# The last four steps of an attention kernel: biases, one output and one sum moved to other places in the engines' queues

## The chip, the cores and the metric

The kernel runs on one core of one Trainium2 chip. Its time is the device time of one execution in microseconds, given as the median over runs. TensorE (PE), VectorE (DVE), ScalarE (ACT), GpSimd (POOL) and SyncE (SP) each work through a queue of instructions in order; SyncE issues most of the transfers.

## The reference

Attention over 8 batches of 512 tokens with 512 features, in 16 heads of 32, all in float32, with a conditioning row added to queries and keys, and the input added to the output:

```python
Q, K, V = split(x @ Wq.T + bq), split(x @ Wk.T + bk), split(x @ Wv.T + bv)
cQ = Q + split(cond @ Wq.T + bq)          # one row per batch, added to all tokens
cK = K + split(cond @ Wk.T + bk)
attn = softmax(einsum('bhqd,bhkd->bhqk', cQ, cK) / sqrt(32))
out = x + merge(einsum('bhqk,bhkd->bhqd', attn, V))
```

## The kernel before

The work is cut into 32 steps, t = 0 to 31: four heads of one batch each, which fill the 128 partitions. One step needs the row maxima of its scores, the exponentials, the product with V, the denominators, and an output of 128 x 512 numbers, in which 32 x 32 blocks are transposed on VectorE. Steps are staggered: while step t takes its exponentials, the scores of step t+1 are made and their maxima taken, and the projections of the next batch run. The order of every engine's instructions is the order in which the code issues them; waits are placed by the framework from what an instruction reads and writes. The eight banks of PSUM are dealt out by a table (`TURNS`, `row`, `at_end`), so the reader of a bank decides when its next writer may start.

The change lies in the end, from step 29 on (`t = T - 3`), where no projections are left. The names and lines that it and the prediction touch:

- `crossed(t, kc, qc, u)` gives TensorE, in turns, the scores of step t for the exponentials of key chunk kc (L1192, L1195) and those of step u for its maxima of query chunk qc (L635). ScalarE takes the exponentials (L1211), VectorE the maxima: two by one head (L1213), then two heads at once (L644).
- `split_max` splits the negated maxima into three bfloat16 parts: a cast, a subtraction, a cast, a subtraction (L696 to L699). `transpose_max` turns them on TensorE (L722) and copies them out (L728); a matmul with ones then adds them to the scores (L738 in `exponentials`, whose score matmuls are L741 and whose exponentials are L752).
- `times_v` (L763) multiplies exponentials by V. `part_of` does so for some key chunks, and its sum leaves PSUM at once: the first time by a copy on ScalarE into `parts[t]` (L1022), the second time by a copy on ScalarE into a spare place (L1016) and an addition on GpSimd (L1017).
- Denominators: up to step 29 they are sums that ScalarE made beside its exponentials; `masked` (GpSimd, L790) and `spread_sums` (TensorE, L800) lay them out and `denominators_of` copies them from PSUM (ScalarE, L1027). For steps 30 and 31 the exponentials of the four key chunks are added (`sum_of`: L1167 for the first two chunks, L1169 for each further one, on VectorE but for one half of step 30, on GpSimd), and `times_ones` (TensorE, L773) adds over the keys. Of step 31, chunks 0 to 2 are added first and chunk 3 goes to TensorE as it is.
- `send_parts(t, den)`: reciprocal (VectorE, L1032), then `send`: transposed (VectorE, L830), multiplied by the reciprocal (GpSimd, L831), added to the input in `xr[t]` (GpSimd, L832). `store` issues four transfers on SyncE (L850).
- `add_bias(u)` adds V's bias to the input `xr[u]` (GpSimd, L209).
- Step 30's output is made by VectorE alone (transposes L1287 and L1292, reciprocal L1290, multiplication L1294, addition of the input L1326) in `y30`, and stored by `store_30` (L1299), two transfers on SyncE and two on ScalarE's queue.
- Step 31's output: the input times the denominators (L1309) is added to the product (L1319, in two halves), TensorE turns it back (L1321) and the denominators too (L854, from a copy that ScalarE makes, L1311); reciprocal (L1329) and multiplication (L1334, two halves) follow, and four transfers (L1341).

Of the kernel before, what the change touches and what calls it, by code (L numbers as in the profile page):

```python
# [12 lines left out]
ALU = mybir.AluOpType  # L13
# [4 lines left out]
def kernel(  # L18
# [38 lines left out]
    nc = tc.nc  # L57
# [5 lines left out]
    HG = P // HD  # L63
    NP = HG // 2
    NS = S // P
# [56 lines left out]
    def banks(i, n=1):  # L122

        row = row_of[0] or [at_end[j] for j in TURNS[turn[0]]]
        j = row[i]
        if n == 1:
            return psum[:, j, :]
        k = row[i + 1]
        return psum[:, j : k + 1 : k - j, :]
# [27 lines left out]
    def spread(a, d, n=1):  # L157

        return a.rearrange("(f j) d -> j f d", j=BL)[:, :, d : d + n * BL]
# [18 lines left out]
    def turned_by_vector(t):  # L178

        return t < T - 1  # L180

    def load_residual(t):

        b, g = divmod(t, G)
        if t == T - 1:

            xr[t] = xT[b][:, g, :]
        elif late:
            xr[t] = late_part(t % 2 * 10 + 2).rearrange("p (f e) -> p f e", e=BL)
            for h in range(HG):  # L190
                nc.sync.dma_start(xr[t][h * BL : (h + 1) * BL], spread(x[b], h * P + g * BL))
        else:
            two = op.tile([P, NB, 2, BL], F32, tag="xr", name=f"xr_{t}", bufs=2)
            twos[t // 2] = two
            for h in range(HG):
                nc.sync.dma_start(
                    two[h * BL : (h + 1) * BL].rearrange("p f c e -> p f (c e)"),
                    spread(x[b], h * P + g * BL, 2),
                )
            for i in range(2):  # L200
                xr[t + i] = two[:, :, i, :]

    def add_bias(t):

        if turned_by_vector(t):
            bias = bvs[:, t % G, :].unsqueeze(1).broadcast_to([P, NB, BL])
        else:
            bias = bvl.broadcast_to([P, S])
        nc.gpsimd.tensor_tensor(xr[t], xr[t], bias, ALU.add)  # L209
# [521 lines left out]
    es = {}  # L731
# [22 lines left out]
    def times_v(t, kc, pt, chunks=range(NS), half=None):  # L754
        b, g = divmod(t, G)
        at = slice(0, S) if half is None else slice(half * HS, (half + 1) * HS)
        cs = slice(0, NS) if half is None else slice(half * 2, half * 2 + 2)
        for j in range(HG):
            if t in BLOCKED:
                e = blocked[t][:, :, cs, j, kc * BL : (kc + 1) * BL].rearrange("p a c e -> p c a e")  # L760
            else:
                e = es[t, kc, j // 2][:, j % 2, at]
            nc.tensor.matmul(  # L763
                pt[j * HD : (j + 1) * HD, at],
                vs[b % 2][:, kc, (g * HG + j) * HD : (g * HG + j + 1) * HD],
                e,
                start=(kc == chunks[0]),
                stop=(kc == chunks[-1]),
            )

    def times_ones(of, pt, start, stop):
        for j in range(HG):
            nc.tensor.matmul(  # L773
                pt[j * HD : (j + 1) * HD, :],
                ones[:, :HD],
                of[j // 2][:, j % 2, :],
                start=start,
                stop=stop,
            )
# [18 lines left out]
    def spread_sums(apart, pd):  # L798
        for h in range(HG):
            nc.tensor.matmul(  # L800
                pd[h * BL : (h + 1) * BL, :NB],
                modulo,
                apart[:, h].rearrange("p c a -> p (c a)"),
                start=True,
                stop=True,
            )
# [31 lines left out]
    def store():  # L838
        while to_store:
            t = to_store.pop(0)  # L840
            b, g = divmod(t, G)
            for h in range(HG):
                r = slice(h * BL, (h + 1) * BL)
                if t < T - 4:
                    nc.sync.dma_start(
                        spread(out[b], h * P + (g - 1) * BL, 2),
                        twos[t // 2][r].rearrange("p f c e -> p f (c e)"),
                    )
                else:
                    nc.sync.dma_start(spread(out[b], h * P + g * BL), xr[t][r])  # L850

    def untranspose(o, pt):
        for qc in range(NS):
            nc.tensor.transpose(  # L854
                pt[:, qc * P : (qc + 1) * P], o[:, qc * P : (qc + 1) * P], ident
            )
# [143 lines left out]
    parts = {}  # L1000
# [3 lines left out]
    def late_part(i):  # L1004
        return late[0][:, i, :]

    def part_of(t, pt, of, between=None):

        for k, kc in enumerate(of):
            if k and between:  # L1010
                between()
            times_v(t, kc, pt, of)
        if t in parts:
            p = late_part(3 + len(parted))
            parted.append(t)
            nc.scalar.copy(p, pt)  # L1016
            nc.gpsimd.tensor_tensor(parts[t], parts[t], p, ALU.add)  # L1017
        else:
            if not parts:
                parts["all"] = stage.tile([P, NC, D], F32, tag="w", name="parts")  # L1020
            parts[t] = parts["all"][:, t % NC, :]
            nc.scalar.copy(parts[t], pt)  # L1022

    def denominators_of(t, pd):

        den = op.tile([P, NB, 1], F32, tag="den", name=f"den_{t}")
        nc.scalar.copy(den, pd[:, :NB].unsqueeze(2))  # L1027
        return den

    def send_parts(t, den):  # L1030
        rec = op.tile([P, NB, 1], F32, tag="recs", name=f"recs_{t}")
        nc.vector.reciprocal(rec, den)  # L1032
        send(t, parts[t], rec)
# [130 lines left out]
    def sum_of(t, to, kc, on, prs=range(NP)):  # L1164
        for pr in prs:
            if kc == 1:
                on.tensor_tensor(to[pr], es[t, 0, pr], es[t, 1, pr], ALU.add)  # L1167
            else:
                on.tensor_tensor(to[pr], to[pr], es[t, kc, pr], ALU.add)  # L1169
# [5 lines left out]
    def row(i):  # L1175
        turn[0] = 8 + i
# [41 lines left out]
    late.append(room("late").rearrange("p g c h s -> p (g c) (h s)"))  # L1218
    t = T - 3
    load_residual(t + 1)  # L1220
    row(4)
    exponentials(t, 0)
    row_max(t + 1, 1)
# [3 lines left out]
    den = denominators_of(t - 1, banks(3))  # L1227
# [7 lines left out]
    row(3)  # L1235
    crossed(t, 3, 0, t + 2)
    part_of(t, banks(2), [0, 1], lambda: transpose_max(t + 1, banks(3), nc.scalar.copy))
    add_bias(t - 1)
    send_parts(t - 1, den)
    store()  # L1240

    t = T - 2
    row(0)
    crossed(t, 0, 1)
    apart = masked(t - 1)
    load_residual(t + 1)
    for u in (t - 1, t, t + 1):
        add_bias(u)
    part_of(t - 1, banks(2), [2, 3])
    spread_sums(apart, banks(1))  # L1250
    den = denominators_of(t - 1, banks(1))
    row(1)
    crossed(t, 1, 2)
    acc = room_for_sums(t)
    sum_of(t, acc, 1, nc.gpsimd, [1])
    part_of(t, banks(2), [0])
    send_parts(t - 1, den)
    store()
    row(2)
    crossed(t, 2, 3)  # L1260
    split_max(t + 1, nc.vector)
# [9 lines left out]
    t = T - 1  # L1271
# [7 lines left out]
    acc2 = room_for_sums(t)  # L1279
# [2 lines left out]
    times_v(t, 1, pv)  # L1282
    pd = bank(5)
    times_ones(acc, pd, True, True)
    sum_of(t, acc2, 2, nc.vector)
    den = late_part(9).rearrange("p (f e) -> p f e", e=BL)
    nc.vector.transpose(den.rearrange("p f e -> p (f e)"), pd)  # L1287

    rec = op.tile([P, NB, 1], F32, tag="recs", name=f"recs_{t - 1}")
    nc.vector.reciprocal(rec, den[:, :, 0:1])  # L1290
    y30 = late_part(13).rearrange("p (f e) -> p f e", e=BL)
    nc.vector.transpose(y30.rearrange("p f e -> p (f e)"), parts[t - 1])  # L1292
    x30 = xr.pop(t - 1)
    nc.vector.tensor_tensor(y30, y30, rec.broadcast_to([P, NB, BL]), ALU.mult)  # L1294

    def store_30(queue, hs):
        b, g = divmod(t - 1, G)
        for h in hs:
            queue.dma_start(spread(out[b], h * P + g * BL), y30[h * BL : (h + 1) * BL])  # L1299
# [2 lines left out]
    times_v(t, 2, pv)  # L1302
    pd = bank(7)
    times_ones(acc2, pd, True, False)
    times_ones([es[t, 3, pr] for pr in range(NP)], pd, False, True)
    times_v(t, 3, pv)

    part_x = late_part(10)
    nc.vector.tensor_tensor(part_x, pd, xr[t], ALU.mult)  # L1309
    den = late_part(11)  # L1310
# [3 lines left out]
    rec = op.tile([P, NS, HG, 1], F32, tag="rec", name="rec")  # L1314
    pi, po = bank(6), [bank(4), bank(2)]
    b, g = divmod(t, G)
    two = [slice(0, HS), slice(HS, S)]
    for i in range(2):
        nc.vector.tensor_tensor(oT[:, two[i]], pv[:, two[i]], part_x[:, two[i]], ALU.add)  # L1319
        for qc in (i * 2, i * 2 + 1):  # L1320
            nc.tensor.transpose(  # L1321
                po[i][:, qc * P : (qc + 1) * P], oT[:, qc * P : (qc + 1) * P], ident
            )
        if i == 0:
            untranspose(den, pi)
    nc.vector.tensor_tensor(y30, y30, x30, ALU.add)  # L1326
    store_30(nc.sync, (0, 1))
    store_30(nc.scalar, (2,))
    nc.vector.reciprocal(  # L1329
        rec, pi.rearrange("p (c h e) -> p c h e", c=NS, h=HG)[:, :, :, 0:1]  # L1330
    )
    for i in range(2):
        cs = slice(i * 2, i * 2 + 2)
        nc.vector.tensor_tensor(  # L1334
# [5 lines left out]
        for c in (i * 2, i * 2 + 1):  # L1340
# [1 line left out]
                out[b].rearrange("(c p) (h g e) -> c g p h e", p=P, h=HG, g=G)[c, g],  # L1342
                y[:, c].rearrange("p (h e) -> p h e", h=HG),
            )
    store_30(nc.scalar, (3,))


# [1 line left out]
_INS = [  # L1349
# [27 lines left out]
```

## Time and profile before

| | |
|---|---|
| time, median of 3 runs (lowest, highest) | 664.89 us (664.83, 665.09) |
| the profiled execution: its own time, its span | 664.89 us, 663.1 us |
| busy share of the span: PE, DVE, ACT, POOL | 98%, 87%, 82%, 51% |
| busy from 609.8 to 632.6 us: PE, DVE, ACT, POOL | 22.8, 16.5, 15.4, 9.0 of 22.8 us |
| 632.6 to 641.4 | 7.6, 7.4, 6.4, 7.9 of 8.8 us |
| 641.4 to 656.1 | 14.7, 14.1, 9.2, 0.0 of 14.7 us |
| 656.1 to 660.4 | 1.1, 2.4, 0.6, 0.0 of 4.3 us |

Times in the profile count from the start of the span. L with a number is a line of the kernel before. A line of a timeline gives start, duration, engine, line, operation, what is written from what, shape, how many instructions are merged, and in brackets the idle time before and what ended it. PEld is TensorE loading weights; SPq and ACTq are the queues from which SyncE and ScalarE issue transfers. A float32 matmul shows as two instructions, one for each of its passes. In the chain of waits, each piece is what the next one waited for.

### The profile page before, as it was taken

Reading aid. Unit: us, or ns where it says so; the run is one execution under the profiler, and the core shown is the slowest. Engines: PE = TensorE matmul, PEld = TensorE weight load, DVE = VectorE, ACT = ScalarE, POOL = GpSimd, SP = SyncE. Lnnn points to the kernel's source line nnn. Section 1 sums busy time; section 2 is a strip of 40 time slices with the busy share of each in tenths; the row PEclk is TensorE's granted clock in tenths of the full one; section 3 lists DMA queues with packets and bytes.
Section 4 is the critical chain, followed back from the end, with each engine's and each line's share of the span. In section 5 each row is a group of like instructions: output and inputs, shape, how many; then the busy total and the mean of one; then the engine's idle time right before and its main releaser. Section 6 shows DMA issues by size and latency. Waiting matters only on the chain.

```text
span 663.1 us, 22865 instructions
## 1 busy us (share of the span) xinstructions
PE 652.7 (98%) x9100; PEld 307.0 (46%) x9100; DVE 578.4 (87%) x845; ACT 543.2 (82%) x1391; POOL 338.0 (51%) x447
## 2 busy tenths in 40 slices
PE   8999999999999999999999999999999999999996
PEld 7454444544445444444544445444544545445431
DVE  5898988989798898979889898998979888897787
ACT  2479797888979888898989889798997978888673
POOL 5642543647537464565635664464744656352360
PEclk9999999999999999999999999999999999999998
DMA  9718548285665838657493865839476573830212
GB/s 210 147 33 211 119 109 211 66 219 118 158 168 123 208 73 222 132 138 184 106 223 74 205 151 129 197 75 233 95 180 154 131 185 67 214 89 16 44 33 33
DMA packets 140815, 90.86 MB, mean 137 GB/s; under 512 B 117436, under 2 KB 126308, under 8 KB 140708
## 3 DMA queue, kind: packets, MB, share of 16 engines
q1 hardware_dynamic: 132196, 73.78, 48.3%
q0 software_dynamic: 5568, 14.95, 8.8%
q8 instruction: 72, 1.18, 0.8%
q10 hardware_dynamic: 2944, 0.66, 0.5%
q14 instruction: 35, 0.29, 0.1%
HBM read 20.27 MB, written 8.39 MB: 43 GB/s over the span
## 4 chain that ended last, share of the span: by engine, by line
PE 94%; DVE 3%; issue 1%; DMA 1%; ACT 1%; ACTq 0%; DVEq 0%
PE psum L469 44%; PE psum L635 19%; PE psum L763 16%; PE psum L741 8%; PE psum L738 3%; PE psum L410 2%; DVE acc L1169 1%; DMA early<-in_x_dram 1%; DVE nmax L644 1%; PE psum L1195 1%; DVE nmax L1213 0%; DVE acc L1167 0%; PE psum L800 0%; PE psum L870 0%; ACT arena L682 0%
## 5 line engine op out<-in xcount | busy, mean ns | idle before, releaser
L602 DVE TENSOR_REDUCE nmax<-psum 128x1 f32<-128x512 f32 x326 | 205.1, 681 | 42.9 <-PE psum L635 42.4
L682 ACT ACTIVATE psum<-psum,nmax 128x512 f32<-128x512 f32 x256 | 169.3, 665 | 46.6 <-DVE nmax L602 34.5
L752 ACT ACTIVATE arena<-psum 128x512 f32<-128x512 f32 x264 | 136.3, 602 | 31.2 <-PE psum L741 22.2
L682 ACT ACTIVATE arena<-psum,nmax 128x512 f32<-128x512 f32 x224 | 152.9, 709 | 4.9 <-issue 4.2
L635 PE MATMUL psum<-kT,qT 32*128 32x512 f32 x1024 | 151.5, 619 | 0.0
L655 DVE STREAM_TRANSPOSE blocks<-blocks 128x1024 f32<-128x1024 f32 x112 | 132.3, 1220 | 0.3 <-DMA blocks<-arena 0.3
L644 DVE TENSOR_REDUCE nmax<-psum 128x2 f32<-128x1024 f32 x87 | 105.5, 1213 | 1.1 <-PE psum L635 1.1
L666 POOL DMA_DIRECT2D blocks<-arena x112 | 55.9, 504 | 72.8 <-ACT arena L682 63.6
L831 POOL TENSOR_TENSOR res<-res,recs 128x512 f32<-128x512 f32 x30 | 31.4, 1047 | 118.8 <-DVE res L830 118.8
L635 PEld LDWEIGHTS psum<-kT,qT 32*128 32x128 f32 x1024 | 55.1, 182 | 62.3 <-issue 17.4
L763 PE MATMUL psum<-arena,v 128*32 128x512 f32 x576 | 69.4, 597 | 0.0
L741 PE MATMUL psum<-qT,kT 32*128 32x512 f32 x528 | 67.9, 587 | 0.0
L682 ACT ACTIVATION_READ_ACCUMULATOR psum<-psum,nmax 128x1 f32 x256 | 52.6, 205 | 0.0
L763 PE MATMUL psum<-blocks,v 128*32 128x256 f32 x896 | 52.1, 381 | 0.0
L682 ACT ACTIVATION_READ_ACCUMULATOR arena<-psum,nmax 128x1 f32 x224 | 50.8, 227 | 0.0
L832 POOL TENSOR_TENSOR xr<-res,xr 128x512 f32<-128x512 f32 x30 | 38.4, 1279 | 2.4
L209 POOL TENSOR_TENSOR xr<-xr,wT_q 128x512 f32<-128x512 f32 x30 | 38.5, 1284 | 0.3
L763 PEld LDWEIGHTS psum<-blocks,v 128*32 128x32 f32 x896 | 26.4, 110 | 25.0 <-ACT arena L752 10.6
L830 DVE STREAM_TRANSPOSE res<-psum 128x512 f32<-128x512 f32 x28 | 20.1, 717 | 19.8 <-issue 16.0
L469 PE MATMUL psum<-wT_v,xT 128*32 128x256 f32 x512 | 34.2, 382 | 0.0
L469 PE MATMUL psum<-wc_v,xc 128*32 128x256 f32 x512 | 33.5, 379 | 0.0
L544 POOL TENSOR_TENSOR v<-v 128x512 f32<-128x512 f32 x14 | 17.9, 1277 | 29.3 <-ACT v L532 29.3
(190 smaller groups left out, 986.4 us busy)
## 6 DMA issues: line engine op xcount, KB each, us to landing
blocks<-arena SPq DMA_DIRECT2D x336, 128.0 KB, 4.1
blocks<-arena POOLq DMA_DIRECT2D x112, 128.0 KB, 4.0
xr<-in_x_dram SPq DMA_DIRECT2D x60, 128.0 KB, 2.7
x<-in_x_dram SPq DMA_DIRECT2D x56, 128.0 KB, 3.5
out_dram<-xr SPq DMA_DIRECT2D x56, 128.0 KB, 2.5
w_q<-in_L_cond_Wq_dram SPq DMA_DIRECT2D x4, 256.0 KB
w_k<-in_L_cond_Wk_dram SPq DMA_DIRECT2D x4, 256.0 KB, 7.3
w_v<-in_L_cond_Wv_dram SPq DMA_DIRECT2D x4, 256.0 KB
```

Of the source, the lines that this page charges most:

```text
L209: nc.gpsimd.tensor_tensor(xr[t], xr[t], bias, ALU.add)
L469: nc.tensor.matmul(pt[r], still[:, r], moving, start=(kc == kcs[0]), stop=(kc == kcs[-1]))
L602: nc.vector.tensor_reduce(nmax[t][:, qc, j : j + 1, 0], pt, AX.X, ALU.max, negate=True)
L635: nc.tensor.matmul(pt, qkT["q", t][r, qc * P : (qc + 1) * P], qkT["k", t][r, :], start=True, stop=True,)
L644: nc.vector.tensor_reduce(nmax[t][:, qc, pr * 2 : pr * 2 + 2, 0], pt, AX.X, ALU.max, negate=True)
L655: nc.vector.transpose(e, e)
L666: queue.dma_start(to.rearrange("p c h s -> p (c h s)"), of)
L682: nc.scalar.activation(to, of, AF.Exp, bias=nmax[t][:, qc, j, :], accum_out=sums[t][:, qc, j, :],)
L741: nc.tensor.matmul(bank[j], qkT["k", t][r, kc * P : (kc + 1) * P], qkT["q", t][r, :], start=False, stop=True,)
L752: nc.scalar.activation(e[:, i, :], bank[pr * 2 + i], AF.Exp)
L763: nc.tensor.matmul(pt[j * HD : (j + 1) * HD, at], vs[b % 2][:, kc, (g * HG + j) * HD : (g * HG + j + 1) * HD], e, start=(kc == chunks[0]), ...
L832: nc.gpsimd.tensor_tensor(xr[t], y, xr[t], ALU.add)
```

## The change

Five edits, all in the last four steps:

- `add_bias` of steps 28, 29 and 31 is issued at the beginning of step 29's part; that of step 30 takes the place that step 28's had. Before, step 28's stood at the end of step 29's part, the three others in the middle of step 30's.
- The second half of step 29's product with V is added to `parts[29]` by VectorE straight from PSUM, in place of ScalarE's copy and GpSimd's addition.
- `send_parts` and `store` of step 29 are issued ahead of the next `crossed`, whose maxima VectorE takes, and ahead of GpSimd's half of `sum_of`.
- Of step 31, the third key chunk's exponentials aren't added on VectorE; TensorE takes them directly, with four matmuls more (eight instructions).
- The input is added to `y30` as soon as that is scaled, and its four transfers are issued there, all on SyncE. In step 31's output the denominators are turned first, and their reciprocal stands between the two halves of the sum.

```diff
-    def part_of(t, pt, of, between=None):
+    def part_of(t, pt, of, between=None, directly=False):
...
-        if t in parts:
+        if directly:
+            nc.vector.tensor_tensor(parts[t], pt, parts[t], ALU.add)
+        elif t in parts:
             p = late_part(3 + len(parted))
             parted.append(t)
             nc.scalar.copy(p, pt)
             nc.gpsimd.tensor_tensor(parts[t], parts[t], p, ALU.add)
...
     t = T - 3
     load_residual(t + 1)
+    load_residual(t + 2)
+    for u in (t - 1, t, t + 2):
+        add_bias(u)
     row(4)
...
     part_of(t, banks(2), [0, 1], lambda: transpose_max(t + 1, banks(3), nc.scalar.copy))
-    add_bias(t - 1)
+    add_bias(t + 1)
     send_parts(t - 1, den)
     store()
...
     apart = masked(t - 1)
-    load_residual(t + 1)
-    for u in (t - 1, t, t + 1):
-        add_bias(u)
-    part_of(t - 1, banks(2), [2, 3])
+    part_of(t - 1, banks(2), [2, 3], directly=True)
     spread_sums(apart, banks(1))
     den = denominators_of(t - 1, banks(1))
+    send_parts(t - 1, den)
+    store()
     row(1)
     crossed(t, 1, 2)
     acc = room_for_sums(t)
     sum_of(t, acc, 1, nc.gpsimd, [1])
     part_of(t, banks(2), [0])
-    send_parts(t - 1, den)
-    store()
...
     times_ones(acc, pd, True, True)
-    sum_of(t, acc2, 2, nc.vector)
     den = late_part(9).rearrange("p (f e) -> p f e", e=BL)
...
     nc.vector.tensor_tensor(y30, y30, rec.broadcast_to([P, NB, BL]), ALU.mult)
+    nc.vector.tensor_tensor(y30, y30, x30, ALU.add)
...
     times_ones(acc2, pd, True, False)
+    times_ones([es[t, 2, pr] for pr in range(NP)], pd, False, False)
     times_ones([es[t, 3, pr] for pr in range(NP)], pd, False, True)
+    store_30(nc.sync, range(HG))
     times_v(t, 3, pv)
...
+    untranspose(den, pi)
     for i in range(2):
         nc.vector.tensor_tensor(oT[:, two[i]], pv[:, two[i]], part_x[:, two[i]], ALU.add)
...
         if i == 0:
-            untranspose(den, pi)
-    nc.vector.tensor_tensor(y30, y30, x30, ALU.add)
-    store_30(nc.sync, (0, 1))
-    store_30(nc.scalar, (2,))
-    nc.vector.reciprocal(
-        rec, pi.rearrange("p (c h e) -> p c h e", c=NS, h=HG)[:, :, :, 0:1]
-    )
+            nc.vector.reciprocal(
+                rec, pi.rearrange("p (c h e) -> p c h e", c=NS, h=HG)[:, :, :, 0:1]
+            )
...
-    store_30(nc.scalar, (3,))
```

## The prediction

> **What bounds the kernel now.** I read the head of the page first, then the chain of waits over the last 31 us, then the timeline of each engine at the places where that chain leaves TensorE.
>
> ```profile
> span 663.1 us, 22865 instructions
> PE 94%; DVE 3%; issue 1%; DMA 1%; ACT 1%; ACTq 0%; DVEq 0%
> ```
>
> ```profile
> 636.22 0.16 DVE recs L1032
> 636.38 0.57 DVE res L830
> 636.95 1.23 DVE nmax L1213 x2
> 638.18 1.19 DVE nmax L644
> ...
> 641.38 0.41 PE psum L722 x4
> ```
>
> The profiled execution took 664.89 us, which is also the median of the runs; its span is 663.1, so 1.8 us lie around it and stay. TensorE carries 94% of the chain. Nothing that the change touches can pay or cost before the chain leaves TensorE, and that happens only in the last 30 us: VectorE's maxima of step 31 (L1213, L644), ending at 639.37, lead to the four transposes L722 at 641.38, for which TensorE stands idle. Columns: start, duration, engine, tile, line.
>
> ```profile
> 11.82 1.26 POOL L393 TENSOR_TENSOR xc<-xT 128x512 f32<-128x512 f32 x1 [6.76 <-DVE xT L908]
> 11.96 1.15 DVE L928 TENSOR_SCALAR bias<-early 128x4 f32<-128x4 f32 x1
> ```
>
> ```profile
> 635.84 2.36 POOL L1167 TENSOR_TENSOR acc<-arena 128x1024 f32<-128x1024 f32 x1
> 638.15 1.05 POOL L831 TENSOR_TENSOR res<-res,recs 128x512 f32<-128x512 f32 x1
> 639.13 1.03 PE L741 MATMUL psum<-qT,kT 32*128 32x512 f32 x8
> 639.28 1.26 POOL L832 TENSOR_TENSOR xr<-res,xr 128x512 f32<-128x512 f32 x1
> 639.39 1.22 DVE L696 CAST split<-nmax 128x16 bf16<-128x16 f32 x1
> 640.86 0.20 DVE L698 CAST split<-rest 128x16 bf16<-128x16 f32 x1
> ```
>
> This is the costliest wait in the region, and it isn't shown as a wait. The cast L696 handles 16 columns in 1.22 us; L698, the same shape, takes 0.20. L696 starts 0.11 us after GpSimd's L832 and ends at 640.61, 0.07 after it (639.28 + 1.26 = 640.54). The same happens at the kernel's start: L928, on four columns, runs to 13.11, GpSimd's L393 to 13.08. So a small VectorE operation of this kind, issued under a GpSimd one, is held until that ends. About 1.02 us of the cast is GpSimd's second operation on step 29's output, and GpSimd is late with it because the 2.36 us sum L1167 stands ahead. TensorE had been free since 639.13 + 1.03 = 640.16.
>
> **The biases.** Three of the four additions (GpSimd, L209) move to 610 us, the one of step 30 replaces that of step 28.
>
> ```profile
> 621.82 1.27 POOL L1017 TENSOR_TENSOR parts<-parts,late 128x512 f32<-128x512 f32 x1 [11.71 <-ACT late L1016]
> ```
>
> GpSimd idles 11.71 us ahead of L1017, and three additions of under 1.3 us are hidden there; the one of step 31 waits for the last projection out of that tile, and the next in GpSimd's queue is this same L1017. Price nothing; without that cover, 3.9 us in front of step 28's output. The slot of step 28's addition, taken by step 30's of the same size, keeps its length. What counts is the other end: at 631-635 us GpSimd no longer has three additions and, with the direct sum, no L1017 ahead of step 29's output.
>
> **Step 29's output ahead of the maxima.**
>
> ```profile
> 630.74 1.92 PE L763 MATMUL psum<-arena,v 128*32 128x512 f32 x16
> 632.64 0.70 PE L635 MATMUL psum<-kT,qT 32*128 32x512 f32 x2
> 633.61 0.38 PE L1192 MATMUL psum<-wT_v,onesb 3*128 3x512 bf16 x2
> 633.80 1.29 DVE L1213 TENSOR_REDUCE nmax<-psum 128x1 f32<-128x512 f32 x2 [1.62 <-PE psum L635]
> 635.77 0.70 PE L635 MATMUL psum<-kT,qT 32*128 32x512 f32 x2
> ...
> 645.75 0.68 DVE L1274 TENSOR_TENSOR parts<-psum,parts 128x512 f32<-128x512 f32 x1
> ```
>
> The new direct addition (VectorE, PSUM and SBUF in) is the same operation and shape as L1274: 0.68. It can start when the matmuls L763 end, 632.66, so 632.70 to 633.38; reciprocal 0.16 and transpose 0.57, with some hundredths between, end at 634.15. VectorE was idle 1.62 us ahead of 633.80, so the maxima behind it start 0.35 us late and end, after their 2.4 us, at 636.57. Who waits? TensorE's L1192 needs the bank that the addition reads, at 633.61; it is released at about 633.43. The next maxima are bound by TensorE: they come 633.80 - 632.64 = 1.16 after its L635, so 635.77 + 1.16 = 636.93, and they started at 636.95 before. So VectorE's 0.7 us of output work leaves the path between the two pairs of maxima and wins nothing: the lateness of 0.35 is swallowed, and the last maximum still ends at 639.37. If the addition cost 0.3 more than its row, the result would be the same; if it cost less it would win nothing either.
>
> GpSimd gains. L831 starts at 634.2, L832 1.13 later (the spacing of 638.15 and 639.28), the sum at 636.6, and it ends at 636.6 + 2.36 = 638.95, 0.4 us before the cast. The cast then costs 0.20: 639.59. From its end to L722 it was 640.61 to 641.38, 0.77, so L722 at 640.36, just behind TensorE's own 640.16. **Gain 1.02.** SP's four stores of step 29 go out some 4 us sooner, in front of nothing.
>
> The Trainium skill, page "SBUF — State Buffer", section "Who interferes with whom", has a rule for this: VectorE's copies and casts, and its two-input operations on SBUF, share a port pair with GpSimd, and whichever is issued second blocks until the first has finished. The two rows above agree, to 0.07 and 0.03 us. The same rule speaks against the new order, in which the longest GpSimd operation stands last before the cast; that is the second rival.
>
> **One sum taken by TensorE.**
>
> ```profile
> 650.89 2.35 DVE L1169 TENSOR_TENSOR acc<-acc,arena 128x1024 f32<-128x1024 f32 x2
> 651.37 1.07 PE L763 MATMUL psum<-arena,v 128*32 128x512 f32 x8
> 653.30 0.11 PEld L773 LDWEIGHTS psum<-acc,wT_q 128*32 128x32 f32 x2 [0.93 <-DVE acc L1169]
> 654.62 1.44 PE L763 MATMUL psum<-arena,v 128*32 128x512 f32 x6
> 655.38 0.68 DVE L1309 TENSOR_TENSOR late<-psum,xT 128x512 f32<-128x512 f32 x1
> ```
>
> From L722 on TensorE is busy without a gap until it waits 0.93 us for L1169 at 653.30. All up to L763 at 651.37 moves by 1.02, to 650.35. Before, 651.37 to the last L763's end, 656.06, was 4.69. Afterwards there is no wait, but one group of eight passes more. A group costs 0.85 (16 in 1.92 against 8 in 1.07): four steps of 0.86 and 1.07 make 4.51. **Gain 0.18**; the edit nearly only swaps a wait for work, bounded by -0.86 (if the wait stayed) and +1.0 (if the matmuls were free). The products end at 654.86.
>
> VectorE is rid of L1169 and free at 649.87 instead of 653.24. What it did for step 30 between there and L1309 (653.24 to 655.38, 2.15) and the addition of step 30's input, 0.68 by L1326 below, then end at 652.7. The denominators of step 31 leave TensorE at 650.35 + 3 x 0.86 + 1.07 = 654.0, so the addition is covered by 1.3 us. L1309 goes from 654.05 to 654.73 and is still ahead of the products.
>
> **The end.**
>
> ```profile
> 656.09 0.59 ACT L1311 COPY late<-psum 128x512 f32<-128x512 f32 x1 [2.50 <-DVE late L1309]
> 656.16 0.76 DVE L1319 TENSOR_TENSOR late<-psum,late 128x256 f32<-128x256 f32 x2
> 656.83 0.68 DVE L1326 TENSOR_TENSOR late<-late 128x512 f32<-128x512 f32 x1
> 656.91 0.60 PE L854 MATMUL psum<-ident,late 128*128 128x128 f32 x4
> 657.55 0.26 DVE L1329 RECIPROCAL rec<-psum 128x16 f32<-128x16 f32 x1
> 657.92 0.76 DVE L1334 TENSOR_TENSOR late<-psum,rec 128x256 f32<-128x256 f32 x2
> ...
> 658.49 1.48 SPq L1341 DMA_DIRECT2D out_dram<-late  x2
> 659.74 0.65 ACTq L1299 DMA_DIRECT2D out_dram<-late  x1
> ```
>
> ```profile
> out_dram<-late SPq DMA_DIRECT2D x4, 64.0 KB, 2.4
> out_dram<-late ACTq DMA_DIRECT2D x4, 64.0 KB, 2.3
> ```
>
> L1319's first half starts at 654.93 instead of 656.16, 1.2 sooner. L1326 was hidden between it and the denominators' transposes L854, so moving it wins nothing here. Those transposes now stand first in TensorE's queue, and wait for ScalarE's copy, which waits for L1309: 654.75 + 0.59, then 0.1 and 0.60 for L854, end at 656.07; queued behind are the output's transposes, which were ready at 655.35. Reciprocal to 656.36, second half of the output to 656.7, its two transposes 0.4, its scaling 0.42 and hand-overs: about 657.6, against 658.68. The reorder gives back 0.1: **1.08 sooner** at this point; between 0.8, if each hand-over takes 0.1 more, and 1.3.
>
> The last transfer was L1299 on ScalarE's queue, issued at 659.74, landing at 662.04; span end minus that, 1.06, stays. Now all four of its kind go out on SP from 652.8 on, where SP's queue holds nothing until the last two stores. The last issue is SP's second, 0.74 (half of 1.48) behind the first, which follows the first half at 657.2: about 658.0, and with the landing of 2.4, 660.4. **Gain 1.65** in all; with a landing 0.3 shorter because fewer transfers queue, 1.95.
>
> **Sum.** 1.02 + 0.18 = 1.2 at the products, 1.08 at the last arithmetic, 1.65 at the last transfer: 664.89 - 1.65 = 663.2. A difference under 0.2%, 1.33 us, can hardly be told from none.
>
> **Rivals.** First: the cast isn't freed, because something else stretched it. Against it stand two pairs of matching ends; for it, no row shows L696 without GpSimd. Then the 1.02 is lost: 664.3, same. Chance 0.10.
>
> Second, slower: GpSimd's 2.36 us sum is late and holds the cast. It stands behind L831, which stands behind VectorE's direct addition. From a start at 637.03 on (forecast 636.6) each tenth late costs a tenth; from 638.7 on all the gain is gone; at 639.3, just ahead of the cast, this ends at 641.7 instead of 640.61, and with the 0.63 us of the other parts the kernel takes 665.3. For it: the margin is only 0.4. Against: every operation in that queue has a measured twin. Chance 0.08, most of it in the partial case, 663.5 to 664.5.
>
> Third: the stores bring nothing at the end, because something else than the last landing closes the program, or the two SP stores land later. Then only 1.08 is won: 663.8, same. For it: SP's own last store, issued at about 659.2 and landing at 661.6, was only 0.45 behind. Chance 0.12.
>
> **Numbers.** The forecast has 0.70, with an own range of 662.6 to 663.6, some of it above 663.56. Faster 0.68, same 0.27, slower 0.05 (the second rival in full, or a wait that I don't see). The range, 662.6 to 664.3, takes in the first and third rival.
>
> **What would show it.** Right: the first cast near 0.2 us with GpSimd idle; L722 near 640.4; maxima at the same time as before; no wait of TensorE for VectorE's sums of step 31; no store of step 30 after 656. Wrong: a cast over 0.5 us, the next-to-last maxima ending after 637, or a span above 662.3.

## The result, and the profile after

The changed kernel takes 663.2 us (median of ten runs, 662.92 to 663.58); the kernel before, run beside it, 664.88. The ratio is 0.9972, with a 95% interval of 0.9963 to 0.998: 0.28% faster, a small difference, but the interval doesn't reach 1. The profiled execution took 663.47 us, 1.42 less than the one of before.

The head of the page and the end of the chain of waits, after (start, duration, engine, tile, line; the changed kernel's lines stand one to five higher from L1016 on, so that GpSimd's sum L1167 is L1169 there):

```profile
span 661.7 us, 22877 instructions
PE 94%; DMA 2%; DVE 1%; SPq 1%; ACT 1%; issue 0%; ACTq 0%; DVEq 0%
```

```profile
637.24 1.23 DVE nmax L1215 x2
638.47 1.19 DVE nmax L644
639.68 0.21 DVE split L696
640.66 0.40 PE psum L722 x4
```

VectorE's share of the chain went from 3% to 1%. The chain still leaves TensorE at the same place, the last maxima, but the piece between them and the transposes L722 is shorter, and `recs` and `res` (L1032, L830), two of its pieces before, are gone from it. The timeline shows why.

```profile
631.03 1.92 PE L763 MATMUL psum<-arena,v 128*32 128x512 f32 x16
633.09 0.69 DVE L1014 TENSOR_TENSOR parts<-psum,parts 128x512 f32<-128x512 f32 x1 [0.62 <-PE psum L800]
633.89 0.71 DVE L830 STREAM_TRANSPOSE res<-parts 128x512 f32<-128x512 f32 x1
634.52 1.25 DVE L1215 TENSOR_REDUCE nmax<-psum 128x1 f32<-128x512 f32 x2
634.68 1.05 POOL L831 TENSOR_TENSOR res<-res,recs 128x512 f32<-128x512 f32 x1 [3.21 <-DVE res L830]
637.04 2.35 POOL L1169 TENSOR_TENSOR acc<-arena 128x1024 f32<-128x1024 f32 x1
637.22 1.29 DVE L1215 TENSOR_REDUCE nmax<-psum 128x1 f32<-128x512 f32 x2 [0.32 <-PE psum L635]
639.68 0.20 DVE L696 CAST split<-nmax 128x16 bf16<-128x16 f32 x1
639.92 0.18 DVE L697 TENSOR_TENSOR rest<-nmax,split 128x16 f32<-128x16 f32 x1
640.66 0.40 PE L722 MATMUL psum<-identb,split 128*128 128x128 bf16 x4 [0.20 <-DVE split L699]
650.65 1.07 PE L763 MATMUL psum<-arena,v 128*32 128x512 f32 x8
654.10 1.04 PE L763 MATMUL psum<-arena,v 128*32 128x512 f32 x8
654.43 0.69 DVE L1313 TENSOR_TENSOR late<-psum,xT 128x512 f32<-128x512 f32 x1 [1.24 <-PE psum L773]
655.80 0.66 PE L854 MATMUL psum<-ident,late 128*128 128x128 f32 x4 [0.65 <-ACT late L1315]
657.45 1.61 SPq L1342 DMA_DIRECT2D out_dram<-late  x2
657.70 0.42 DVE L1335 TENSOR_TENSOR late<-psum,rec 128x256 f32<-128x256 f32 x1 [0.28 <-PE psum L1326]
```

The first line is the anchor for what follows. The first `times_v` of step 29's second product (L763, sixteen instructions) is issued by unchanged code, yet it starts at 630.74 in the execution of before and at 631.03 in this one; over all profiled executions of this study it starts between 630.62 and 631.47. So executions differ by up to 0.85 us before the change can count; they part mostly in the first 35 us, and drift apart by up to 0.18 more until 631 us, which is 0.01 in 30 us. I therefore read every profile from this anchor (A), and take the span from the trace to the hundredth (663.10 before, 661.68 after), where the page rounds it to a tenth. Before: L722 at A + 10.64, end of the span at A + 32.36. After: A + 9.63 and A + 30.65. By that measure the change brings 1.01 us at L722 and 1.71 us at the end. The medians differ by 1.68.

### The profile page after: what moved, and what is told of

It is laid out like the page before. It is cut to its first block, busy times and chain, and to the rows that moved or that the text cites. A ratio compares the mean times of both kernels' runs of the same rounds, so it can differ in the third digit from the quotient of the medians.

```text
span 661.7 us, 22877 instructions
## 1 busy us (share of the span) xinstructions
PE 653.5 (99%) x9108; PEld 307.8 (47%) x9108; DVE 575.8 (87%) x844; ACT 542.2 (82%) x1390; POOL 337.0 (51%) x446
## 4 chain that ended last, share of the span: by engine, by line
PE 94%; DMA 2%; DVE 1%; SPq 1%; ACT 1%; issue 0%; ACTq 0%; DVEq 0%
PE psum L469 44%; PE psum L635 19%; PE psum L763 17%; PE psum L741 8%; PE psum L738 3%; DMA w_k<-in_L_cond_Wk_dram 1%; SPq L254 1%; PE psum L1197 1%; PE psum L410 1%; PE psum L773 1%; DMA early<-in_x_dram 0%; DVE nmax L644 0%; PE psum L800 0%; ACT arena L682 0%; DVE nmax L1215 0%
## 5 line engine op out<-in xcount | busy, mean ns | idle before, releaser
L752 ACT ACTIVATE arena<-psum 128x512 f32<-128x512 f32 x264 | 136.3, 603 | 30.4 <-PE psum L741 22.3
L831 POOL TENSOR_TENSOR res<-res,recs 128x512 f32<-128x512 f32 x30 | 31.4, 1048 | 122.0 <-DVE res L830 122.0
L763 PE MATMUL psum<-arena,v 128*32 128x512 f32 x576 | 68.5, 597 | 0.0
L763 PE MATMUL psum<-blocks,v 128*32 128x256 f32 x896 | 52.1, 381 | 0.0
L832 POOL TENSOR_TENSOR xr<-res,xr 128x512 f32<-128x512 f32 x30 | 38.5, 1282 | 2.4
L763 PEld LDWEIGHTS psum<-blocks,v 128*32 128x32 f32 x896 | 26.3, 110 | 25.0 <-ACT arena L752 10.6
L830 DVE STREAM_TRANSPOSE res<-psum 128x512 f32<-128x512 f32 x28 | 20.1, 717 | 19.7 <-issue 16.0
```

The costliest lines, as they stand in the source:

```text
L752: nc.scalar.activation(e[:, i, :], bank[pr * 2 + i], AF.Exp)
L763: nc.tensor.matmul(pt[j * HD : (j + 1) * HD, at], vs[b % 2][:, kc, (g * HG + j) * HD : (g * HG + j + 1) * HD], e, start=(kc == chunks[0]), ...
L832: nc.gpsimd.tensor_tensor(xr[t], y, xr[t], ALU.add)
```

## Experiments

Each kernel was profiled once and timed in turn with the kernel before, whose median was 665.05 to 665.23 beside the kernels from e1 on. The last two columns are of its profile.

| kernel | time, us | ratio to before (95%) | L722, after A | span end, after A |
|---|---|---|---|---|
| before | 664.88 | 1 | 10.64 | 32.36 |
| after | 663.2 | 0.9972 (0.9963 to 0.998) | 9.63 | 30.65 |
| e1_output | 664.15 | 0.9983 (0.9974 to 0.9992) | 9.63 | 31.36 |
| e2_sum | 665.35 | 1.0004 (0.9995 to 1.0013) | 10.64 | 32.22 |
| e3_stores | 665.33 | 1.0002 (0.9993 to 1.0011) | 10.65 | 32.55 |
| e9_no_end | 663.98 | 0.9984 (0.9975 to 0.9993) | 9.63 | 31.19 |
| e4_tail | 663.52 | 0.9975 (0.9966 to 0.9984) | 9.62 | 30.71 |
| e5_read | 664.11 | 0.9987 (0.9978 to 0.9996) | 10.19 | 31.20 |
| e6_write | 664.16 | 0.9987 (0.9978 to 0.9996) | 10.51 | 31.54 |
| e7_copy | 664.16 | 0.9988 (0.9979 to 0.9997) | 10.45 | 31.46 |
| e10_bias | 663.29 | 0.997 (0.996 to 0.998) | 9.63 | 30.64 |
| e11_act_cast | 664.93 | 0.9996 (0.9987 to 1.0005) | 10.49 | 32.13 |
| e8_copy_first | 663.19 | 0.9972 (0.9961 to 0.9982) | 9.63 | 30.47 |
| e12_half | 663.32 | 0.9968 (0.9957 to 0.998) | 9.63 | 30.39 |

### The parts alone

**e1_output**: edits one to three (biases, direct addition, step 29's output ahead of the maxima) put into the kernel before.

```diff
+    for u in (t - 1, t, t + 2):
+        add_bias(u)
...
-    part_of(t - 1, banks(2), [2, 3])
+    part_of(t - 1, banks(2), [2, 3], directly=True)
     spread_sums(apart, banks(1))
     den = denominators_of(t - 1, banks(1))
+    send_parts(t - 1, den)
+    store()
```

> Only the biases, the direct addition and step 29's output ahead of the maxima; step 31's sum and the end as before. Theory (GpSimd held the cast, and the rest of the gain comes from other edits): the cast L696 takes 0.20 us, the four transposes L722 come 9.6 us after step 29's second product starts (10.64 in the kernel before), TensorE still waits about 0.9 us for VectorE's sums of step 31, and the whole end moves by 1.02: 663.9 us. Rival (the stores made the gain; the cast is short only because something else changed): 664.9, with the last store's landing as late as before.

L722 comes 1.01 us sooner, the end of the span 1.00. This is most of the gain.

**e2_sum**: edit four (the third chunk's sum by TensorE) alone in the kernel before.

```diff
-    sum_of(t, acc2, 2, nc.vector)
...
     times_ones(acc2, pd, True, False)
+    times_ones([es[t, 2, pr] for pr in range(NP)], pd, False, False)
```

> Only the sum of step 31's third chunk taken by TensorE. Theory: the wait of 0.93 us goes, four matmuls of 0.86 come, so the products of step 31 end 0.18 us sooner and VectorE is done with step 30 some 2.3 us sooner without use: 664.7 us. Rival (the wait was hidden anyway, TensorE is the bound): 0.86 us slower, 665.7. Rival (VectorE's chain was the bound and is shorter by 2.35): 663 or less.

By the trace the products end 0.19 us sooner (A + 25.13 in place of A + 25.32) and the span 0.14; the time can't tell it from nothing.

**e3_stores**: edit five (step 30's addition and stores sooner, the new order of the tail) alone in the kernel before.

```diff
     nc.vector.tensor_tensor(y30, y30, rec.broadcast_to([P, NB, BL]), ALU.mult)
+    nc.vector.tensor_tensor(y30, y30, x30, ALU.add)
...
+    store_30(nc.sync, range(HG))
```

> Only the end: input added to step 30's output at once, its four stores there on SyncE, the denominators of step 31 turned first. VectorE still has the sums of step 31, so that the addition now stands in its queue ahead of the denominators' product, where VectorE is 0.2 us late already. Theory: that product starts 0.65 us later, the last arithmetic ends 1.0 us later than before, the stores of step 30 no longer stand last: about the same as before, 664.9 to 665.2 us. Rival (the end is set by the stores alone): 0.6 us faster, 664.3.

The end is 0.19 us later by the trace; the time can't tell it from before. Its timeline:

```profile
655.38 0.69 DVE L1295 TENSOR_TENSOR late<-late 128x512 f32<-128x512 f32 x1
655.99 0.68 DVE L1311 TENSOR_TENSOR late<-psum,xT 128x512 f32<-128x512 f32 x1
656.70 0.59 ACT L1313 COPY late<-psum 128x512 f32<-128x512 f32 x1 [3.23 <-DVE late L1311]
658.93 1.62 SPq L1340 DMA_DIRECT2D out_dram<-late  x2
```

VectorE is still busy with the sum that edit four takes away, so the moved addition (L1295) stands in front of the input times the denominators (L1311), which starts at A + 25.37 in place of A + 24.64. That costs 0.73 at the tail; what the earlier stores win gives back some 0.5 of it.

**e9_no_end**: edits one to four, without the fifth.

> Biases, direct addition, step 29's output ahead and the sum by TensorE, but the end as before. Theory (the sum alone is worth 0.15 us and the end alone loses 0.2, because VectorE's chain of step 30 leads the end unless the sum has left it; together they are worth 0.74): without the end the kernel wins 1.02 and 0.15, so span minus the start of step 29's second product is 31.25 us (32.36 before, 30.67 with all edits), 1.1 us faster than before. Rival (the sum's removal frees what the end then uses, whatever its order): 30.9 or less.

With 31.19 the table can be added up. Edits one to three: 1.00. Four after them: 0.17. Five after them: 0.54. Edits four and five are worth +0.14 and -0.19 alone, and 0.71 together. In e9_no_end the last issue is a store of step 30 on ScalarE's queue, as it was before:

```profile
658.73 0.65 ACTq L1300 DMA_DIRECT2D out_dram<-late  x1
```

That is A + 27.84. In the changed kernel the last issue is the second of SP's two at 657.45, about 0.8 behind the first: A + 27.2. These 0.6 us of the last issue are what the fifth edit's 0.54 at the end comes from.

### What holds the cast

The prediction put 1.02 us down to GpSimd holding a small VectorE cast. The rival was that something else stretched it. Two kernels add a useless GpSimd instruction behind its sum in the changed kernel, so that it is running when the cast starts: **e5_read** an addition, **e6_write** an instruction that reads nothing.

```diff
     sum_of(t, acc, 1, nc.gpsimd, [1])
+    nc.gpsimd.tensor_tensor(late_part(7), xr[T - 1], xr[T - 1], ALU.add)   # e5_read
+    nc.gpsimd.memset(late[0][:, 6:9, :], 0.0)                             # e6_write
```

> The changed kernel with one more GpSimd operation, which nothing uses, right behind its sum for step 30: an addition of 128x512 read from on-chip memory, 1.27 us. Theory (a GpSimd operation that is running holds VectorE's cast to its end): GpSimd is then busy from 8.3 to 9.6 us after step 29's second product starts, the cast comes at 8.65 and is held to 9.6, about 0.95 us instead of 0.20; the transposes L722 come at 10.4 instead of 9.63, and the whole is 0.75 us slower than the changed kernel. Rival (the cast was long for another reason): cast 0.20, no change.

> The same place, but the additional GpSimd operation only writes: zeros into 128x1536, about 1.3 us. If GpSimd's hold is on the whole port pair, the cast is held as with the addition: 0.9 us or more. If it is only on reading, the cast takes 0.20 us and nothing changes.

e5_read, timeline:

```profile
639.23 1.04 POOL L1260 TENSOR_TENSOR late<-xT 128x512 f32<-128x512 f32 x1
639.56 0.77 DVE L696 CAST split<-nmax 128x16 bf16<-128x16 f32 x1
641.10 0.40 PE L722 MATMUL psum<-identb,split 128*128 128x128 bf16 x4 [0.77 <-DVE split L699]
```

e6_write, timeline:

```profile
639.30 1.37 POOL L1260 MEMSET late<- 128x1536 f32 x1
639.65 1.09 DVE L696 CAST split<-nmax 128x16 bf16<-128x16 f32 x1
641.51 0.40 PE L722 MATMUL psum<-identb,split 128*128 128x128 bf16 x4 [1.09 <-DVE split L699]
```

GpSimd ends at 640.27 and 640.67, the cast at 640.33 and 640.74: 0.06 and 0.07 behind, close to the 0.07 and 0.03 of the two pairs in the prediction. Holding it brings back 0.56 and 0.88 us at L722, and 0.55 and 0.89 at the end. The added addition took 1.04 us and not the 1.27 of L832, so L722 came at 10.19 and not at the forecast 10.4; the mechanism stands, the size of the added load was off. That an instruction which reads nothing holds the cast as well rules out that GpSimd's reads alone do it.

Look at how this shows in a profile: the cast has no idle time ahead of it and no releaser. All of the hold stands in its own duration, 0.77 or 1.09 us in place of 0.20.

**e11_act_cast**: the kernel before, with the first cast of step 31 on ScalarE, to get round GpSimd without moving the output.

```diff
-        on.tensor_copy(sp[:, :, :, 0:1], m)
+        (nc.scalar.copy if t == T - 1 else on.tensor_copy)(sp[:, :, :, 0:1], m)
```

> The kernel before, with only the first cast of step 31's maxima moved to ScalarE, which is idle there. GpSimd's last operation runs until 9.8 us after step 29's second product starts, as before. If GpSimd holds only casts, the split goes on at 8.9 and L722 comes at about 9.8, 0.8 us sooner. If it holds subtractions with both operands in on-chip memory too (the page SBUF, State Buffer, of the Trainium skill says so), the subtraction L697 takes 0.9 us in place of 0.19 and L722 comes at 10.45, 0.2 us sooner than before.

```profile
639.56 1.27 POOL L832 TENSOR_TENSOR xr<-res,xr 128x512 f32<-128x512 f32 x1
639.71 0.26 ACT L696 CAST split<-nmax 128x16 bf16<-128x16 f32 x1 [0.23 <-POOL res L831]
640.00 0.87 DVE L697 TENSOR_TENSOR rest<-nmax,split 128x16 f32<-128x16 f32 x1 [0.37 <-ACT split L696]
```

ScalarE's cast takes 0.26 under the same GpSimd instruction, so ScalarE isn't held. But the subtraction behind it, which reads two tiles from SBUF, now takes 0.87 where it takes 0.18 to 0.19 elsewhere, and ends at 640.87, 0.04 behind GpSimd. The hold only moves on by one instruction: L722 at 10.49, 0.15 sooner than before. GpSimd's work has to be out of the way of the subtraction too.

The Trainium skill, page "SBUF — State Buffer", section "Who interferes with whom", agrees with these three runs, with the numbers beside it. It says that VectorE's copies and casts can use a second pair of ports that it shares with GpSimd, that a subtraction with two SBUF inputs contends with a GpSimd instruction that reads, and that the one issued second blocks until the first is done. It also names ScalarE among those that wait for nobody; 0.26 under L832 fits that.

**e7_copy**: the changed kernel with ScalarE's copy and GpSimd's addition in place of VectorE's direct addition.

```diff
-    part_of(t - 1, banks(2), [2, 3], directly=True)
+    part_of(t - 1, banks(2), [2, 3])
```

> The changed kernel with step 29's second sum taken as before, by ScalarE's copy and GpSimd's addition, while its output stays ahead of the maxima. Theory: VectorE's transpose waits for the GpSimd addition until about 4.0 us after step 29's second product starts (2.9 in the changed kernel), holds the maxima in its queue, which hold TensorE's next scores: the last maximum ends 0.8 us later, L722 at 10.4 instead of 9.63, 0.75 us slower than the changed kernel. Rival (the direct addition is of no use, all is in the order): L722 at 9.63, same time.

```profile
633.62 1.27 POOL L1019 TENSOR_TENSOR parts<-parts,late 128x512 f32<-128x512 f32 x1 [2.22 <-ACT den L1029]
634.92 0.71 DVE L830 STREAM_TRANSPOSE res<-parts 128x512 f32<-128x512 f32 x1 [1.02 <-POOL parts L1019]
639.17 1.22 DVE L644 TENSOR_REDUCE nmax<-psum 128x2 f32<-128x1024 f32 x1
```

The transpose L830 now waits 1.02 us for GpSimd, VectorE's maxima behind it are late, and the last one ends at 640.39 (A + 9.43) in place of A + 8.61. The cast is free, 0.20 at 640.42, but 0.8 us late: L722 at 10.45. So the new order pays only with the direct addition; the copy and addition in front of the maxima cost 0.81 of the 1.71. The reverse, the direct addition in the old order, was not run.

**e10_bias**: the changed kernel with the biases at their old places.

```diff
-    for u in (t - 1, t, t + 2):
-        add_bias(u)
...
+    for u in (t - 1, t, t + 1):
+        add_bias(u)
     part_of(t - 1, banks(2), [2, 3], directly=True)
```

> The changed kernel with the additions of the biases at their old places, three of them at 631 us. Theory (their place matters little, since GpSimd then waits for VectorE's transpose): GpSimd is free of them 3.9 us after step 29's second product starts, its multiplication starts 0.25 us later than in the changed kernel, its sum ends within 0.1 us of the cast; L722 at 9.63 to 9.75, the same time as the changed kernel within 0.1 us. Rival (the biases' place made the gain): L722 at 10 or later.

```profile
634.57 1.05 POOL L831 TENSOR_TENSOR res<-res,recs 128x512 f32<-128x512 f32 x1
636.92 2.36 POOL L1169 TENSOR_TENSOR acc<-arena 128x1024 f32<-128x1024 f32 x1
639.36 0.20 DVE L696 CAST split<-nmax 128x16 bf16<-128x16 f32 x1
```

Nothing changes at L722, and at the end only 0.01. L831 starts at A + 3.86 in place of A + 3.65, so GpSimd's sum ends 0.08 us ahead of the cast (636.92 + 2.36 = 639.28), where the changed kernel leaves about 0.3. Moving the biases buys margin and no time.

### The end

**e4_tail**: the changed kernel with the order of the tail before.

```diff
-    untranspose(den, pi)
     for i in range(2):
...
-            nc.vector.reciprocal(...)
+            untranspose(den, pi)
+    nc.vector.reciprocal(...)
```

> The changed kernel with the order of the last transposes and of VectorE's last operations put back: output's first half, denominators, then the reciprocal after both halves of the sum. Theory (the prediction gave 0.1 us back for this reorder, the trace shows 0.3): TensorE turns the first half while ScalarE copies the denominators, the last arithmetic ends 0.35 us sooner than in the changed kernel, 662.85 us. Rival (the copy of the denominators is last either way): 663.2.

```profile
657.20 0.76 DVE L1335 TENSOR_TENSOR late<-psum,rec 128x256 f32<-128x256 f32 x2
657.65 1.59 SPq L1342 DMA_DIRECT2D out_dram<-late  x2
```

The last arithmetic ends at 657.96, A + 26.78 (657.20 + 0.76), 0.31 us sooner than in the changed kernel (657.70 + 0.42 = 658.12, A + 27.09), but the span ends 0.06 later. The first half's stores start at A + 26.47, against A + 26.42 after. Each of the two queues issues a first and then a second store, and the second waits only for the first: SP's two take 1.6 us together. What sets the end is the first half's time, and that the old order doesn't improve. My expectation, which went by the last arithmetic, missed.

**e8_copy_first**: the changed kernel, with ScalarE's copy of the denominators ahead of VectorE's product, which then reads the copy.

```diff
-    nc.vector.tensor_tensor(part_x, pd, xr[t], ALU.mult)
     nc.scalar.copy(den, pd)
+    nc.vector.tensor_tensor(part_x, den, xr[t], ALU.mult)
```

> The changed kernel with the two readers of step 31's denominators exchanged: ScalarE's copy first, and VectorE's product with the input taken from that copy. Theory (the stores of the first half set the end, and they wait for the denominators' copy, transposes and reciprocal): transposes start 0.7 us sooner, the first half of the sum 0.5 later, the first half's stores 0.3 us sooner, 0.3 us faster than the changed kernel. Rival (the sum of the first half is then last): no gain or 0.2 us slower.

```profile
654.38 0.58 ACT L1314 COPY late<-psum 128x512 f32<-128x512 f32 x1 [1.56 <-PE psum L773]
654.99 0.69 DVE L1315 TENSOR_TENSOR late<-late,xT 128x512 f32<-128x512 f32 x1 [1.86 <-ACT late L1314]
657.20 1.62 SPq L1342 DMA_DIRECT2D out_dram<-late  x2
```

In the changed kernel ScalarE's copy waits for VectorE's product (0.69 us at 654.43), and the transposes L854 wait for the copy. Turned round, the first half's stores go out at A + 26.23, 0.19 sooner, and the span ends 0.18 sooner. The times don't tell the two kernels apart (a ratio of 0.9972 for both).

**e12_half**: e8_copy_first, with heads 0 and 1 of the third chunk's sum on VectorE again, and only those of heads 2 and 3 on TensorE (four instructions fewer).

```diff
+    sum_of(t, acc2, 2, nc.vector, [0])
...
-    times_ones(acc2, pd, True, False)
-    times_ones([es[t, 2, pr] for pr in range(NP)], pd, False, False)
+    for of, js, start in ((acc2, (2, 3), True), ([None, es[t, 2, 1]], (2, 3), False), (acc2, (0, 1), True)):
+        for j in js:
+            nc.tensor.matmul(
+                pd[j * HD : (j + 1) * HD, :], ones[:, :HD], of[j // 2][:, j % 2, :], start=start, stop=False
+            )
```

> A version meant to beat both: the changed kernel with ScalarE's copy of the denominators first, and with half of the third chunk's sum of step 31 back on VectorE (heads 0 and 1), taken by TensorE last, so that TensorE has two matmuls less. Theory (TensorE is the bound from L722 on, VectorE has over 1 us to spare there): the products end 0.43 us sooner than in the changed kernel, the stores 0.24 more: 0.6 us faster than the changed kernel, span minus the start of step 29's second product 30.0 us. Rival (VectorE's chain of step 30 becomes the bound again): 30.4 or more.

```profile
651.98 1.06 PE L1309 MATMUL psum<-acc,wT_q 128*32 128x512 f32 x8
652.84 0.60 PE L1309 MATMUL psum<-arena,wT_q 128*32 128x512 f32 x2
653.27 0.60 PE L1309 MATMUL psum<-arena,wT_q 128*32 128x512 f32 x2
653.30 0.99 PE L773 MATMUL psum<-arena,wT_q 128*32 128x512 f32 x4
654.16 1.42 PE L763 MATMUL psum<-arena,v 128*32 128x512 f32 x6
655.42 0.69 DVE L1319 TENSOR_TENSOR late<-late,xT 128x512 f32<-128x512 f32 x1 [0.66 <-ACT late L1318]
```

The same stretch in e8_copy_first:

```profile
651.47 1.04 PE L773 MATMUL psum<-acc,wT_q 128*32 128x512 f32 x8
652.33 1.90 PE L773 MATMUL psum<-arena,wT_q 128*32 128x512 f32 x16
654.05 1.04 PE L763 MATMUL psum<-arena,v 128*32 128x512 f32 x8
```

A miss: the span ends at A + 30.39, not at the expected 30.0, and only 0.08 sooner than in e8_copy_first. Four instructions fewer save nothing at the products: from the first line to the last product it is 655.58 - 651.98 = 3.60 us with 28 instructions (six more stand between the quoted lines of TensorE), and 655.09 - 651.47 = 3.62 with 32. The instructions of heads 2 and 3 (652.84, 653.27) start 0.43 apart, and the next ones (653.30, of L773) start beside them and not behind; in e8_copy_first four of all heads also take 0.43. What fits is that the matmuls of the four heads, each of which writes 32 partitions of its own, run beside each other, so that the products take as long as the heads that still have all their work; heads 2 and 3 had. That reading was not tested by itself. The rival's 30.4 came out, but not by VectorE's chain, which waits 0.66 us for ScalarE's copy.

## Why the prediction was right, point by point

**The cast.** 0.20 us, and L722 at A + 9.63, where 9.62 was predicted (640.36 - 630.74). Shown by e5_read, e6_write and e11_act_cast to be GpSimd's hold, and by e7_copy to need the direct addition. The first rival has fallen.

**The maxima.** The lateness is swallowed, as predicted: the second pair starts at A + 6.19 (predicted 6.19, 636.93), bound by TensorE, and the last maximum ends at A + 8.61 (predicted 8.63). The direct addition started at A + 2.06, predicted 1.96. The profile names L800 as what released it, but it names L800 for the copy of before too (L1016, at 632.73, A + 1.99), and the code issues both ahead of L800; where the 0.1 us comes from stays open, and it is hidden.

**GpSimd's sum.** It ends 0.3 us ahead of the cast (637.04 + 2.35 = 639.39, cast at 639.68), 0.4 predicted. The second rival, that it holds the cast, had the mechanism right, as e5_read shows, and the place wrong.

**The biases.** Price nothing, right (e10_bias): even their old place is hidden once the addition L1019 of step 29 is gone.

**One sum by TensorE.** 0.18 predicted at the products, 0.19 there alone and 0.20 behind the first three edits (0.14 and 0.17 at the end of the span); the products end at 655.14, A + 24.11, predicted 24.12. What the prediction only mentioned as cover is its larger part: without it the fifth edit costs 0.19 (e3_stores) in place of winning 0.54.

**The end.** 1.65 predicted, 1.71 by the trace. One term was mis-sized on the way: the last arithmetic ends at A + 27.09, where A + 26.86 was predicted (657.6), because the reorder gives back 0.3 (e4_tail) and not 0.1. It changes nothing, because the last issue follows the first half's store, at A + 26.42 against 26.46 predicted. That had some luck in it: the last arithmetic ends only 0.1 us ahead of SP's second store (A + 27.2), so a little later it would have counted. That the median meets the forecast of 663.2 to the tenth is luck as well, for the median of the kernel before moved from 664.88 to 665.23 between the series of runs. The third rival, that the stores bring nothing, has fallen (e9_no_end).

## What to carry to other kernels

A small VectorE instruction that takes several times its usual time in one place, without a wait in front, is worth a look at what GpSimd is doing under it: if the two ends agree to a tenth, move GpSimd's work and not the victim, and look at the next instruction before you move the victim to another engine. Price the parts of a change together as well as alone: here one edit that is worth 0.14 us and one that costs 0.19 win 0.71, since the first frees the engine on which the second puts its work. At the end of a kernel, follow each queue's issues back to what releases the first of them; arithmetic behind that point can become faster without any gain.

## What the runs showed of the hardware that I had not expected

- A GpSimd instruction that reads nothing, the memset of 128x1536, held a VectorE cast of 16 columns to 1.09 us.
- GpSimd's addition of a 128x512 tile to itself took 1.04 us; of two different tiles (L832) 1.27.
- In e12_half, matmuls on two of the four groups of 32 partitions followed each other every 0.43 us, no faster than four on all of them in e8_copy_first.
- SP needs about 0.8 us for each of the last stores (1.61 for two), ScalarE's queue 0.66 (1.32 for two), so the second issue of a queue came after all arithmetic, in the changed kernel by 0.1 us, in e4_tail by 0.4.
